# A token layer's chunk is issued in another order, beside and after another layer's convolutions

## The chip, the core and the metric

The kernel runs on one core of one Trainium2 chip, as one launch. The metric is device time in microseconds (us). The kernel before took 7097.66 us, the median of 3 runs between 7095.06 and 7098.18. The execution that the profiler recorded took 7082.74 us.

## The reference, cut to what matters

The input is `x` of 4 batches, 48 channels, 256 x 256 pixels, in float32. Four layers follow each other, each as `x = x + layer(groupnorm(x))`.

- Layer 0 is channel attention: a 1x1 and a 3x3 depthwise convolution make q, k and v; a 48 x 48 softmax of q against k weights v, and a 1x1 projection follows. Once the softmax of a batch is known, all of what lies behind it is one 3x3 convolution of the normalized input.
- Layer 1 is the token layer. It reads a batch's memory as tokens of 48 numbers, whatever pixels they came from:

```python
t = x.reshape(B, H * W, dim)
t = gelu(gelu(t @ W1 + b1))                 # 48 -> 16, exact gelu
x1, x2 = t[..., :8], t[..., 8:]
n = layernorm(x2)                           # over 8 features
sp = depthwise3x3(n as an image) + dw_b
ch = conv1x1(n as an image) + pw_b
out = (x1 * (sp * ch)) @ W2 + b2            # 8 -> 48, added to x
```

- Layers 2 and 3 are scans: each line of the image gets a 5-tap convolution of the line before it, down, up, right and left.

A layer starts with a group norm over whole batches, so layer 2 of a batch cannot start before layer 1 of that batch has ended. The scans take all four batches together.

## The kernel before

**Stages.** Layer 0's sums for the softmax of all batches fill the time from 0 to about 1050 us. Then come layer 0's output convolutions: 64 blocks of 16 rows, 16 a batch. `block(u)` (L623) makes one block in two halves. A half is two calls of `full` (L630, 3 matmuls each, `py` L642) and one of `rest(q)` (L646, 6 matmuls on half of the array, L651), then for each of its two PSUM tiles an addition of the input (DVE, L665) and statistics for the next group norm (DVE, L666). Half 0 writes two tiles of the PSUM pool `spare` (2 banks), half 1 two of the pool `banks` (5 banks). Between blocks ScalarE normalizes the next block's rows, `x1n` and `x2n` (L599), each in a single buffer, after the matmuls that read the old ones.

The blocks of batch 0 run alone. From about 1186 us the blocks of batches 1 to 3 run between the pieces of the token layer, whose 32 chunks (8 a batch, 32 rows each) follow one batch behind. When the blocks are used up (about 2359 us), the rest of the chunks runs alone until about 2737 us, and the scans take the rest. I call the first of these the **mixed stage**, the second the **lone stage**.

**A tick.** `tick(c, conv, alone)` (L985) works on three chunks: it transposes chunk c+1, makes the features of chunk c, and the output of chunk c-2 (`old`). `alone` is true when no half block is left. The pieces of one chunk are

- `load` (L799): two DMAs of 768 KB bring the chunk's tokens into `tok`, which has one buffer; `relay` (L807): GpSimd copies them to `pairs`, one buffer.
- `transposed(c, i)` (L814), i from 0 to 5: TensorE turns a sixth (4 matmuls into a bank, `ptok` L818); odd i are copied out by ScalarE (L822), even i by DVE (L824), into `xt`.
- `hidden` (L828): the projection `t @ W1` for each half of the features, 8 matmuls `ph` (L765); the eighth reads the `xt` of i = 5. ScalarE applies the two gelus (L835, L844, L846).
- `centered` (L849): a matmul `pm` (L852) makes the mean, DVE subtracts it (L854), GpSimd squares (`sq`, L856).
- `normed` (L858): a matmul `pvar` (L861), ScalarE's square root `v` (L863), DVE's reciprocal (L864) and product (L866), and ScalarE writes the image `n` (L868). Then ScalarE's queue starts four DMAs of 8 KB, `near<-n` (L878 to L887): each chunk's first and last row goes to its neighbours.
- `shift` (L889): GpSimd makes three shifted copies `nears` of a chunk's `near` (L891). That of chunk c-2 needs the third DMA of chunk c-1.
- `gate` (L893): three matmuls over `n` (`psp`, L897), one over `nears` (L898), one for the 1x1 convolution (`pch`, L900); then ScalarE (L903), DVE (L904) and GpSimd make the product `g` (L906).
- `output(c, ip, alone)` (L923), ip 0 and 1: four matmuls `pout` (L936), each on a quarter of the array's rows and each in a bank of its own, eight additions of the input `xr` on DVE (L946), eight copies of `y` to `yr` on GpSimd (L951), and after ip 1 the store `x2r<-yr` (L963) on SP's queue. `add_b2` (L919) has ScalarE add the bias to `xr`, which `load_x` (L908) loads.
- `finish` (L975): statistics on DVE (L979).

A mixed tick holds four half blocks. Its pieces stand in this order: the two `hidden`, `gate` of c-2, half block A, `centered`, transposes 0 and 1, `output` 0, half block B, transposes 2 and 3, `normed`, `output` 1, half block C, transposes 4 and 5, half block D. A and C are halves 0 and write `spare`.

**What sets the order.** The Tile framework records the pieces, and a scheduler of its own model of time lays down each engine's instructions in a fixed sequence; pieces given earlier have priority, but one that its model finds not ready is passed. On the chip each engine then runs its sequence in order. PSUM has eight banks: 5 `banks`, 2 `spare`, 1 for small things.

Of the kernel before, what the change touches and what calls it, by code (L numbers as in the profile page):

```python
# [9 lines left out]
F32 = mybir.dt.float32  # L10
# [8 lines left out]
P = 96  # L19
# [102 lines left out]
def layers01(ctx, tc, x, xp, xe, inside, pick, xc, x1, wqk, dwqk, wv, dwv, projT, temp, k, coef, coef1, gated, spare):  # L122
# [496 lines left out]
    stats = {}  # L619
    ends = []  # L620
    unwritten = []

    def block(u):  # L623

        b, n = items[u]
        if n == 0:
            stats[b] = small_p.tile([P, NB * 4, 6], F32, tag="st", name="st")
        held = {}

        def full(c):  # L630
            if c == 0:
                if u + 1 < len(items):
                    ahead_[u + 1] = load(items[u + 1])
                while unwritten:
                    unwritten.pop(0)()
                held["ps"] = {}
                held["w"] = [wy[b, i].rearrange("p x r o -> p x (r o)") for i in range(2)]
            ps = (banks if c % 2 else spare).tile([P, 2, W], F32, tag="bank", name="py")
            held["ps"][c] = ps
            x1n = ready[u][0]  # L640
            for dx in range(3):
                nc.tensor.matmul(  # L642
                    ps, lhsT=held["w"][0][:, dx], rhs=x1n[:, 2 * c : 2 * c + 2, dx : dx + W], start=dx == 0, stop=False
                )

        def rest(q):  # L646
            x2n = ready[u][1]
            for dx in range(3):
                for s in range(2):
                    here = slice(64 * s, 64 * s + 64)  # L650
                    nc.tensor.matmul(  # L651
                        held["ps"][q + 2 * s],
                        lhsT=held["w"][1][here, dx],
                        rhs=x2n[here, 2 * q : 2 * q + 2, dx : dx + W],
                        start=False,
                        stop=dx == 2,
                    )
            if q == 0:
                held["y"] = big.tile([P, M, W], F32, tag="y", name="y", bufs=2)
            elif u + 1 < len(items):  # L660
                ready[u + 1] = normed(items[u + 1], ahead_[u + 1])
            t1 = ahead_[u][0]
            for c in (q, q + 2):
                part = held["y"][:, 2 * c : 2 * c + 2, :]
                nc.vector.tensor_add(part, held["ps"][c], t1[:P, 2 * c : 2 * c + 2, :])  # L665
                nc.vector.bn_stats(stats[b][:, n * 4 + c, :], part.rearrange("p h w -> p (h w)"))  # L666
            if q == 0:
                return
            dst = x1[b].rearrange("c (h w) -> c h w", w=W)
# [21 lines left out]
        some_late()  # L691
    sctx.close()

    tick, n_ticks = gated(ctx, tc, banks, p_small)
    todo = [(u, q) for u in range(NB, len(items)) for q in range(2)]
    made = {}

# [15 lines left out]
            piece()  # L713


def gated_layer(ctx, tc, banks, p_small, x1, x2r, w1, w2, dw, ends, pw, cols, b2, k, coef1, coef2):

# [131 lines left out]
    def centered(c):  # L849
# [5 lines left out]
        sq = sqs[c] = feat.tile([128, CH], F32, tag="sq", name="sq", bufs=1)  # L855
        nc.gpsimd.tensor_mul(sq, d, d)  # L856

    def normed(c):  # L858
        b, j = items[c]
# [3 lines left out]
        nc.scalar.activation(v, pv, AF.Sqrt, bias=eps)  # L863
        nc.vector.reciprocal(v, v)  # L864
        d = ds.pop(c)
        nc.vector.tensor_mul(d, d, v)  # L866
        n = n_sb[c % NN]
        nc.scalar.activation(  # L868
            n[:, :, 1 : W + 1].rearrange("p k (t q) -> p k q t", q=4),
            by_token(d),  # L870
            AF.Identity,
            bias=col[:, 3:4],
            scale=col[:, 2:3],
        )

        here, a, z = near[c % NN], slice(0, F), slice(F, 2 * F)
        top, last = n[0:F], n[128 - F : 128]
        nc.scalar.dma_start(here[a, 1, :], last[:, 0, :])  # L878
        nc.scalar.dma_start(here[z, 0, :], top[:, 1, :])
        if j == 0:  # L880
            nc.scalar.dma_start(here[a, 0, :], zeros)
        else:
            nc.scalar.dma_start(near[(c - 1) % NN][z, 1, :], top[:, 0, :])
        if j == NJ - 1:
            nc.scalar.dma_start(here[z, 1, :], zeros)
        else:
            nc.scalar.dma_start(near[(c + 1) % NN][a, 0, :], last[:, 1, :])  # L887
# [35 lines left out]
    def output(c, ip, alone):  # L923
        b, j = items[c]
        if ip == 0:

            yrs[c] = res.tile([P, 8, 4, 128], F32, tag="yr", name="yr")
            if j == 0:
                stats[b] = feat.tile([P, NJ * 8, 6], F32, tag="st", name="st1")
        y = ys[c, ip] = res.tile([P, 2, 4, W], F32, tag="y1", name="y1")  # L930
        t, g = xrs[c, ip], gs[c]
        ps = []
        for q in range(4):
            p = banks.tile([P, 2, W], F32, tag="bank", name="pout")
            here = slice(32 * q, 32 * q + 32)
            nc.tensor.matmul(  # L936
                p,
                lhsT=w2_sb[here, ip, :],
                rhs=g[here],
                start=True,  # L940
                stop=True,
            )
            ps.append(p)
        for q in range(4):
            for kk in range(2):
                nc.vector.tensor_add(y[:, q % 2, 2 * kk + q // 2, :], ps[q][:, kk], t[:, 4 * kk + q, :])  # L946
        if alone:
            load_x(c + 1, ip)
        for i2 in range(2):
# [16 lines left out]
                )  # L966

        unwritten.append(write)
        if alone:
            unwritten.pop()()  # L970

    after = []
    unwritten = []
# [11 lines left out]
    def tick(c, conv, alone):  # L985
# [30 lines left out]
        if was:  # L1016
            pieces.append(lambda: gate(old))
        pieces.append(conv)
        if now:
            pieces.append(lambda: centered(c))  # L1020
        if new:
            pieces += [lambda i=i: transposed(c + 1, i) for i in range(2)]
        if was:
            pieces += [lambda: [add_b2(old, ip) for ip in range(2)], lambda: output(old, 0, alone)]
        pieces.append(conv)
        if new:
            pieces += [lambda i=i: transposed(c + 1, i) for i in range(2, 4)]
        if was:
            pieces.append(lambda: finish(old, 0))
        if now:  # L1030
            pieces.append(lambda: normed(c))
        if was:
            pieces.append(lambda: output(old, 1, alone))
        pieces.append(conv)
        if new:
            pieces += [lambda i=i: transposed(c + 1, i) for i in range(4, NI)]
        if was:
            pieces.append(lambda: finish(old, 1))
        pieces += [conv, last]
# [506 lines left out]
def program(ctx, tc, a, out, at):  # L1546
# [13 lines left out]
    def gated(ctx, tc, banks, p_small):  # L1560
        names = ("w1", "w2", "dw", "ends", "pw", "cols", "b2")
        to = [coef2[:, b] for b in range(B)]
        return gated_layer(ctx, tc, banks, p_small, x1, x2r, *(a[n] for n in names), k, coefs[1], to)
# [141 lines left out]
```

## Time and profile before

| What | Value |
|---|---|
| profiled execution | 7082.74 us, span 7080.7 us |
| runs | 7095.06, 7097.66, 7098.18 us |
| mixed ticks with all pieces, 1338.0 to 2358.9 us | 20 ticks, 51.0 us each |
| lone stage, 2358.9 us to the last store at 2736.4 us | 377.5 us |
| scans from the first matmul at 2745.2 us | 4335 us |
| TensorE busy over the span | 6631.8 us, 94% |
| DVE, ScalarE, GpSimd busy | 3644.3, 1854.5, 2086.7 us |

PE is TensorE's matmuls, PEld its weight loads, ACT is ScalarE, POOL is GpSimd, and SPq and ACTq are DMA issues on the queues of SyncE and ScalarE. L897 is line 897 of the kernel before. A line of the timeline gives start in us, duration in us, engine, line, operation, tiles, shapes, the count that was merged and, in brackets, the idle time before it and what ended that. PEclk is the granted clock of TensorE as a share of full speed. A line of the waits gives who waited for whom, the total in us, how often, and the longest.

### The profile page before, as it was taken

Reading aid. Unit: us, or ns where it says so; the run is one execution under the profiler, and the core shown is the slowest. Engines: PE = TensorE matmul, PEld = TensorE weight load, DVE = VectorE, ACT = ScalarE, POOL = GpSimd, SP = SyncE. Lnnn points to the kernel's source line nnn. Section 1 sums busy time; section 2 is a strip of 40 time slices with the busy share of each in tenths; the row PEclk is TensorE's granted clock in tenths of the full one; section 3 lists DMA queues with packets and bytes.
Section 4 is the critical chain, followed back from the end, with each engine's and each line's share of the span. In section 5 each row is a group of like instructions: output and inputs, shape, how many; then the busy total and the mean of one; then the engine's idle time right before and its main releaser. Section 6 shows DMA issues by size and latency. Waiting matters only on the chain.

```text
span 7080.7 us, 133914 instructions
## 1 busy us (share of the span) xinstructions
PE 6631.8 (94%) x55886; PEld 5328.3 (75%) x55886; DVE 3644.3 (51%) x8754; ACT 1854.5 (26%) x2166; POOL 2086.7 (29%) x4211
## 2 busy tenths in 40 slices
PE   4999999999999866999998999987899999899999
PEld 3766643333333325999998999986898999899999
DVE  6777623455555554444444445754344444444444
ACT  2440012344444443443441000001354344000000
POOL 0000000233333455330002556663000000455777
PEclk9999999999999877999999999998999999999999
DMA  7752145566666676995577778988997466865775
GB/s 195 188 151 82 52 134 155 166 188 184 192 183 183 153 175 193 278 299 143 184 215 185 199 196 163 254 241 210 186 165 134 130 193 188 221 191 176 274 289 203
DMA packets 1177647, 1325.90 MB, mean 187 GB/s; under 512 B 831344, under 2 KB 1006064, under 8 KB 1124688
## 3 DMA queue, kind: packets, MB, share of 16 engines
q1 hardware_dynamic: 1164016, 1229.16, 64.3%
q10 hardware_dynamic: 12928, 87.83, 3.7%
q8 instruction: 439, 7.19, 0.4%
q14 instruction: 168, 1.38, 0.1%
q0 software_dynamic: 96, 0.33, 0.0%
HBM read 793.94 MB, written 522.19 MB: 186 GB/s over the span
## 4 chain that ended last, share of the span: by engine, by line
PE 57%; SPq 3%; DMA 3%; DVE 2%; POOL 1%; issue 1%; ACT 1%; ACTq 0%; POOLq 0%; DVEq 0%
PE ps L1151 56%; SPq L1187 2%; DMA D<-d 1%; DMA tok<-x 1%; ACT d L1226 1%; POOL s L1436 1%; DVE y L946 0%; POOL yr L951 0%; PE ph L765 0%; DVE v L864 0%; DMA near<-n 0%; DVE st L979 0%; DMA r<-R 0%; PE pout L936 0%; PE psp L897 0%
## 5 line engine op out<-in xcount | busy, mean ns | idle before, releaser
L1151 PE MATMUL ps<-d,w 128*128 128x128 f32 (+1 forms) x18360 | 2071.2, 276 | 99.7 <-DVE d L1157 61.9
L1151 PEld LDWEIGHTS ps<-d,w 128*128 128x128 f32 x18360 | 2066.4, 193 | 104.3 <-DVE d L1157 65.7
L1151 PE MATMUL ps<-r,w 128*128 128x128 f32 (+1 forms) x18360 | 2072.1, 276 | 68.9 <-POOL r L1368 35.7
L1151 PEld LDWEIGHTS ps<-r,w 128*128 128x128 f32 x18360 | 2066.3, 193 | 74.7 <-DVE r L1157 37.5
L1157 DVE SCALAR_TENSOR_TENSOR d<-ps,b,d 128x128 f32<-128x128 f32 x3054 | 979.3, 348 | 1154.0 <-PE ps L1151 1073.8
L1436 POOL TENSOR_TENSOR s<-s,r 128x128 f32<-128x128 f32 x1536 | 748.6, 522 | 332.4 <-DVE r L1157 329.9
L1157 DVE SCALAR_TENSOR_TENSOR r<-ps,b,pre 128x128 f32<-128x128 f32 x1530 | 489.9, 348 | 582.2 <-PE ps L1151 581.3
L1157 DVE SCALAR_TENSOR_TENSOR r<-ps,b,r 128x128 f32<-128x128 f32 x1530 | 489.8, 348 | 460.0 <-PE ps L1151 429.7
L324 PE MATMUL acc<-moving,raw 128*32 128x240 f32 (+1 forms) x6144 | 687.9, 382 | 11.5 <-DVE moving L307 11.5
L642 PE MATMUL py<-x1n,wy 128*96 128x512 f32 x1536 | 696.6, 602 | 1.9
L1368 POOL COPY pre<-c 128x128 f32<-128x128 f32 x1530 | 559.8, 405 | 467.5 <-DVE r L1157 464.7
L324 PE MATMUL acc<-moving,still 128*32 128x240 f32 (+1 forms) x6144 | 684.5, 382 | 6.0 <-DVE still L311 2.3
L1226 ACT ACTIVATE d<-x,spread 128x256 f32<-128x256 f32 x752 | 511.2, 827 | 544.0 <-DMA D<-d 378.1
L1307 ACT COPY u<-d 128x384 f32<-128x384 f32 x510 | 451.3, 904 | 570.7 <-DVE d L1157 509.7
L324 PEld LDWEIGHTS acc<-moving,raw 128*32 128x32 f32 x6144 | 431.5, 110 | 185.6 <-DVE moving L307 11.8
L642 PEld LDWEIGHTS py<-x1n,wy 128*96 128x96 f32 x1536 | 243.7, 164 | 413.8 <-issue 371.0
L1368 POOL COPY r<-c 128x128 f32<-128x128 f32 x6 | 2.4, 399 | 1688.9 <-DMA c<-U 1688.9
L665 DVE TENSOR_TENSOR y<-py,t 96x512 f32<-96x512 f32 x256 | 173.2, 676 | 558.8 <-PE py L651 558.8
L324 PEld LDWEIGHTS acc<-moving,still 128*32 128x32 f32 x6144 | 371.8, 110 | 35.8 <-DVE still L311 3.2
L951 POOL COPY yr<-y 96x256 f32<-96x256 f32 x512 | 316.4, 662 | 201.6 <-DVE y L946 191.1
L651 PE MATMUL py<-x2n,wy 64*96 64x512 f32 x1536 | 360.8, 601 | 0.0
L651 PEld LDWEIGHTS py<-x2n,wy 64*96 64x96 f32 x1536 | 116.5, 158 | 233.4 <-issue 229.3
(204 smaller groups left out, 4213.8 us busy)
## 6 DMA issues: line engine op xcount, KB each, us to landing
t<-in_xc SPq DMA_DIRECT2D x64, 1536.0 KB
c<-U SPq DMA_DIRECT2D x348, 256.0 KB
D<-d SPq DMA_DIRECT2D x54, 1536.0 KB
d<-D SPq DMA_DIRECT2D x54, 1536.0 KB
R<-r SPq DMA_DIRECT2D x54, 1536.0 KB
r<-R ACTq DMA_DIRECT2D x54, 1536.0 KB
U<-u SPq DMA_DIRECT2D x84, 768.0 KB
raw<-in_xp SPq DMA_DIRECT2D x36, 1728.0 KB
```

The source lines that it names most:

```text
L324: nc.tensor.matmul(out[32 * i : 32 * i + 32, : n * C], lhsT=still[i][:, first : first + 32], rhs=moving[:, i, lo : lo + n * C], start=u == ...
L642: nc.tensor.matmul(ps, lhsT=held["w"][0][:, dx], rhs=x1n[:, 2 * c : 2 * c + 2, dx : dx + W], start=dx == 0, stop=False)
L651: nc.tensor.matmul(held["ps"][q + 2 * s], lhsT=held["w"][1][here, dx], rhs=x2n[here, 2 * q : 2 * q + 2, dx : dx + W], start=False, stop=dx ...
L665: nc.vector.tensor_add(part, held["ps"][c], t1[:P, 2 * c : 2 * c + 2, :])
L951: nc.gpsimd.tensor_copy(yrs[c][:, :, 2 * i2 + ip, :].rearrange("p j (n a g) -> p j n a g", a=4, g=4)[:, :, :, al], y[:, i2, al].rearrange( ...
L1151: nc.tensor.matmul(ps[m][:, here], lhsT=w[:, n, :], rhs=old[:, q, there], start=first, stop=last)
L1157: nc.vector.scalar_tensor_tensor(new[:, m], ps[m], bias[:, m : m + 1], inp[:, m], ALU.add, ALU.add)
L1187: queues[q % len(queues)].dma_start(v[p0 : p0 + np_, m, 8 * n0 : 8 * n1], src[c0:c1, 8 * n0 : 8 * n1, at : at + 64])
L1226: pin(nc.scalar.activation(dst, src, AF.Identity, bias=g[:, 1:2], scale=g[:, 0:1]))
L1307: nc.scalar.copy(v[:, :, i, :, al], line)
L1368: nc.gpsimd.tensor_copy(dst[:, m].rearrange("p (J a b) -> p J a b", J=NBK, b=B), v[:, m, j, :, gl].rearrange("p J b a -> p J a b"),)
L1436: nc.gpsimd.tensor_add(v, v, line[:, m].rearrange("p (J a b) -> p J a b", J=NBK, b=B))
```

## The change

Only the order of work and two choices of buffers change; every chunk is computed as before. In both stages:

- `gate` of c-2 still follows `hidden`, and `add_b2` stands right behind it.
- `normed` now ends with the square root; the reciprocal, the product and `n` are a piece of their own, `scaled`, and the four `near` DMAs another, `neighbours`. Both stand at the end of the tick, behind half block D and the last transpose.
- `output` is given in two parts of two `pout` each.
- The statistics of a half block (L666) are held back in the list `behind` until the next half block's first `full`.

In the mixed stage `output` 0 follows half block A and `centered`, transposes 0, 1, 3, 4, 2 stand together behind B, `pvar` and `output` 1 follow C, and transpose 5 follows D. In the lone stage every second `pout` takes a bank of `spare`, `output` 1 takes its `y` from the pool `big`, which layer 0 used until then, and a chunk's store stands behind the load of the next tokens, where it was issued as soon as it was made.

```diff
         def full(c):
+            if c < 2:
+                while behind:
+                    behind.pop(0)()
...
                 nc.vector.tensor_add(part, held["ps"][c], t1[:P, 2 * c : 2 * c + 2, :])
-                nc.vector.bn_stats(stats[b][:, n * 4 + c, :], part.rearrange("p h w -> p (h w)"))
+                behind.append(
+                    lambda c=c, part=part: nc.vector.bn_stats(
+                        stats[b][:, n * 4 + c, :], part.rearrange("p h w -> p (h w)")
+                    )
+                )
...
         nc.scalar.activation(v, pv, AF.Sqrt, bias=eps)
+        vs[c] = v
+
+    def scaled(c):
+        v = vs.pop(c)
         nc.vector.reciprocal(v, v)
         d = ds.pop(c)
         nc.vector.tensor_mul(d, d, v)
...
+    def neighbours(c):
+        b, j = items[c]
+        n = n_sb[c % NN]
         here, a, z = near[c % NN], slice(0, F), slice(F, 2 * F)
         top, last = n[0:F], n[128 - F : 128]
         nc.scalar.dma_start(here[a, 1, :], last[:, 0, :])
...
-        y = ys[c, ip] = res.tile([P, 2, 4, W], F32, tag="y1", name="y1")
...
+        if i == 0:
+            if alone and ip:
+                ys[c, ip] = big.tile([P, 2, 4, W], F32, tag="y", name="y1", bufs=2)
+            else:
+                ys[c, ip] = res.tile([P, 2, 4, W], F32, tag="y1", name="y1")
...
-        for q in range(4):
-            p = banks.tile([P, 2, W], F32, tag="bank", name="pout")
+        for q in (2 * i, 2 * i + 1):
+            ps[q] = (spare if alone and q % 2 else banks).tile([P, 2, W], F32, tag="bank", name="pout")
...
         unwritten.append(write)
-        if alone:
-            unwritten.pop()()
...
         def last():
             if c + 2 < n:
                 load(c + 2)
+            while alone and unwritten:
+                unwritten.pop(0)()
...
+        pieces += of_old(gate)
+        if alone:
+            pieces += [conv] + of_now(centered) + turned(0, 1) + added + out(0)
+            pieces += turned(3, 4) + of_old(finish, 0) + of_now(normed) + out(1) + turned(2, 5)
+        else:
+            pieces += [*added, conv, *of_now(centered), *out(0), conv]
+            pieces += turned(0, 1, 3, 4, 2) + of_old(finish, 0)
+            pieces += [conv, *of_now(normed), *out(1), conv, *turned(5)]
+        pieces += of_now(scaled) + of_now(neighbours) + of_old(finish, 1)
+        pieces.append(last)
```

More of the change, by code (lines that the diff above doesn't have):

```diff
@@ L621, in layers01 @@
     unwritten = []
+    behind = []
     def block(u):
@@ L665, in rest @@
                 nc.vector.tensor_add(part, held["ps"][c], t1[:P, 2 * c : 2 * c + 2, :])
-                nc.vector.bn_stats(stats[b][:, n * 4 + c, :], part.rearrange("p h w -> p (h w)"))
+                behind.append(
[3 more added lines that the diff above has]
+                )
             if q == 0:
                 return
+            while behind and n == NB - 1:
+                behind.pop(0)()
             dst = x1[b].rearrange("c (h w) -> c h w", w=W)
@@ L692, in layers01 @@
     sctx.close()
-    tick, n_ticks = gated(ctx, tc, banks, p_small)
+    tick, n_ticks = gated(ctx, tc, banks, p_small, big)
     todo = [(u, q) for u in range(NB, len(items)) for q in range(2)]
@@ L713, in layers01, with gated_layer @@
             piece()
-def gated_layer(ctx, tc, banks, p_small, x1, x2r, w1, w2, dw, ends, pw, cols, b2, k, coef1, coef2):
+def gated_layer(ctx, tc, banks, p_small, big, spare, x1, x2r, w1, w2, dw, ends, pw, cols, b2, k, coef1, coef2):
     nc = tc.nc
@@ L856, in centered @@
         nc.gpsimd.tensor_mul(sq, d, d)
+    vs = {}
     def normed(c):
-        b, j = items[c]
         pv = banks.tile([128, CH], F32, tag="bank", name="pvar")
@@ L921, in add_b2, with output @@
         nc.scalar.activation(t, t, AF.Identity, bias=b2_sb)
-    def output(c, ip, alone):
+    def output(c, ip, i, alone):
         b, j = items[c]
-        if ip == 0:
+        if ip == 0 and i == 0:
             yrs[c] = res.tile([P, 8, 4, 128], F32, tag="yr", name="yr")
@@ L929, in output @@
                 stats[b] = feat.tile([P, NJ * 8, 6], F32, tag="st", name="st1")
-        y = ys[c, ip] = res.tile([P, 2, 4, W], F32, tag="y1", name="y1")
-        t, g = xrs[c, ip], gs[c]
-        ps = []
-        for q in range(4):
-            p = banks.tile([P, 2, W], F32, tag="bank", name="pout")
+        if i == 0:
[3 more added lines that the diff above has]
+                ys[c, ip] = res.tile([P, 2, 4, W], F32, tag="y1", name="y1")
+        y, t, g = ys[c, ip], xrs[c, ip], gs[c]
+        ps = {}
+        for q in (2 * i, 2 * i + 1):
+            ps[q] = (spare if alone and q % 2 else banks).tile([P, 2, W], F32, tag="bank", name="pout")
             here = slice(32 * q, 32 * q + 32)
             nc.tensor.matmul(
-                p,
+                ps[q],
                 lhsT=w2_sb[here, ip, :],
@@ L942, in output @@
             )
-            ps.append(p)
-        for q in range(4):
+        for q in ps:
             for kk in range(2):
                 nc.vector.tensor_add(y[:, q % 2, 2 * kk + q // 2, :], ps[q][:, kk], t[:, 4 * kk + q, :])
+        if i == 0:
+            return
         if alone:
@@ L1015, in tick @@
             pieces += [lambda: hidden(c, 1), lambda: hidden(c, 0)]
[L1016 to L1039, printed above, removed]
+        turned = lambda *which: [lambda i=i: transposed(c + 1, i) for i in which] if new else []
+        out = lambda ip: [lambda i=i: output(old, ip, i, alone) for i in range(2)] if was else []
+        of_now = lambda f: [lambda: f(c)] if now else []
+        of_old = lambda f, *more: [lambda: f(old, *more)] if was else []
+        added = of_old(lambda c: [add_b2(c, ip) for ip in range(2)])
+        pieces += of_old(gate)
[8 more added lines that the diff above has]
+        pieces.append(last)
         if c == n + 1:
@@ L1558, in program, with gated @@
     x2r = [dram.tile([8 * C, 8, 1024], F32, tag=f"x2r_{b}", name=f"x2r_{b}") for b in range(B)]
-    def gated(ctx, tc, banks, p_small):
+    def gated(ctx, tc, banks, p_small, big):
         names = ("w1", "w2", "dw", "ends", "pw", "cols", "b2")
         to = [coef2[:, b] for b in range(B)]
-        return gated_layer(ctx, tc, banks, p_small, x1, x2r, *(a[n] for n in names), k, coefs[1], to)
+        return gated_layer(ctx, tc, banks, p_small, big, spare, x1, x2r, *(a[n] for n in names), k, coefs[1], to)
     names = ("wqk", "dwqk", "wv", "dwv", "projT", "temp")
```

## The prediction, made before the result

> **What bounds the kernel now.** I read the page's slices first, for whether TensorE sets the time everywhere.
>
> ```profile
> span 7080.7 us, 133914 instructions
> ...
> PE   4999999999999866999998999987899999899999
> ...
> PEclk9999999999999877999999999998999999999999
> ```
>
> A slice is 177 us. TensorE is full nearly everywhere. The gap in slices 14 and 15 is the lone stage (2358.9 to 2736.4 us). The change touches only the mixed ticks left of that gap and the gap itself. Next I read each engine's busy time by stage (mixed ticks, lone stage, its last 90 us).
>
> ```profile
> core 0: us, PE busy (x) PEld busy (x) DVE busy (x) ACT busy (x) POOL busy (x), PEclk, DMA share, GB/s
> 1338.00:2307.80 969.80, 960.84 (x3484) 359.39 (x3482) 540.86 (x933) 398.05 (x385) 329.37 (x590) 0.99 0.68 186
> 2358.90:2646.20 287.30, 193.93 (x788) 78.36 (x786) 160.82 (x295) 127.68 (x147) 145.58 (x199) 0.81 0.70 160
> 2646.20:2736.40 90.20, 49.73 (x114) 16.01 (x114) 41.83 (x88) 22.88 (x21) 41.92 (x67) 0.63 0.51 139
> ```
>
> In the mixed ticks TensorE is idle for 9 us of 970: any wait put in front of it there lengthens the tick by its whole length, and only fewer or shorter TensorE stretches shorten it. In the lone stage no engine is full; a chain of waits sets the time. Of the waits of the mixed stage, two matter, both on the small DMAs `near`:
>
> ```profile
> POOL nears L891 <- DMA near<-n: 106.9, 14, 12.3
> ...
> ACT xt L822 <- DMA near<-n: 47.9, 10, 5.8
> ```
>
> They cost nothing today, since TensorE has other work. How much room they have, the timelines of ScalarE, DVE, GpSimd and TensorE in the tick of 1712 us tell.
>
> ```profile
> 1726.44 3.35 DVE L864 RECIPROCAL v<-v 128x512 f32<-128x512 f32 x1 [1.32 <-ACT v L863]
> ```
> ```profile
> 1730.70 1.34 ACT L868 ACTIVATE n<-d,col 128x512 f32<-128x512 f32 x1 [4.29 <-DVE d L866]
> 1732.07 0.66 ACTq L878 DMA_DIRECT2D near<-n  x1
> 1732.77 0.63 ACTq L879 DMA_DIRECT2D near<-n  x1
> 1733.44 0.63 ACTq L883 DMA_DIRECT2D near<-n  x1
> 1734.10 3.48 ACTq L887 DMA_DIRECT2D near<-n  x1
> 1737.62 0.59 ACT L822 COPY xt<-ptok 128x512 f32<-128x512 f32 x1 [5.58 <-DMA near<-n]
> ```
> ```profile
> 1742.24 1.91 POOL L891 COPY nears<-near 16x512 f32<-16x512 f32 x3 [9.30 <-DMA near<-n]
> ```
> ```profile
> 1725.49 7.09 PE L642 MATMUL py<-x1n,wy 128*96 128x512 f32 x12
> ...
> 1752.32 1.02 PE L898 MATMUL psp<-nears,ends_sb 80*128 80x512 f32 x2
> ```
>
> The reciprocal starts 1 us into half block C; the third `near` issue ends at 1734.07, `nears` starts 8.2 us later and ends at 1744.15, and TensorE asks for it (L898) at 1752.32. Two half blocks' time lies between, with 8 us of slack here, about 6 us as the median of the ticks. From the third issue's end to `nears` the mixed ticks show 4.5 to 9.1 us, median 6.6; the lone ones 4.3 to 6.3.
>
> **Mixed tick, what is saved.** I compared the two fixed sequences engine by engine. A `pout` today waits for a bank, so 4 take 2.0 us behind A's work and 3.0 behind B's; on banks long free, 4 take 1.0. But B must wait for the bank of `pm`, free when DVE has written `d`, 2.75 us after A (4.0 today, with two transposes at 1.0). Behind B the five transposes take 2.4. Behind C, `pvar` and four `pout` take 2.0, and D waits until 3.35 for its bank, held until DVE's additions have read it. Transpose 5 takes 0.45. Without any new wait that is 8.95 us between half blocks against 9.8: a gain of 0.85 us per tick.
>
> **Mixed tick, what is new.** The reciprocal does not stand "behind the sums" in the sequence: it is between two groups of additions. I count from T, the end of half block C. DVE: two additions and two statistics (0.59 to 0.72 and 0.61 each) 2.5; four additions at 0.34 to 3.9; reciprocal 3.3 to 7.2; four additions to 8.55; product 0.65 to 9.2. ScalarE: `n` 1.35 to 10.6. Then the sequence has `x1n` (2.05, to 12.65) **ahead of** the four `near` issues: the third ends at 14.6, the fourth at 15.25 if it takes 0.65 (today it often takes 3 us and more, as in the line above: then 17.6). Then `x2n` 1.23 and the copy of transpose 5, 0.56: `xt` is ready at T+17.05 (19.4).
>
> TensorE: D runs from 3.35 to 11.4, transpose 5 to 11.85. The eighth `ph` reads that `xt` and is due at 13.45: **a first stall of 3.6 us** (6.0 with the slow fourth issue). Today the transposes stood ahead of D, and D covered their copies.
>
> GpSimd: in its sequence the first `nears` copy waits for `near`, and `relay` (two copies, 2.87 us) is between the first `nears` and the other two. With the median 6.6 us `near` lands at 21.2; 0.63 + 2.87 + 1.28 make `nears` ready at T+26.0 (23.7 with 4.3 us, 28.5 with 9.1). Without stalls TensorE would ask at 18.1 (11.85 + `ph` 3.5 + `psp` 2.75), with the first stall at 21.7: **a second stall of 4.3 us**. All of the 7.9 us is TensorE's, for conv A is queued behind L898. While GpSimd's `nears` waits, `relay` and so the next transposes queue behind it; those come behind half block B now, 16 us later, and are not late.
>
> From T to the next T: 26.0, L898 and `pch` 1.8, A 8.0, gap 2.75, B 8.1, transposes 2.4, C 8.1: 57.15 us. To this comes the granted clock. In the lone stage, the idle stretch from 2466.9 to 2469.1 us is followed by this stretch:
>
> ```profile
> 2469.70:2473.10 3.40, 3.40 (x17) 0.50 0.01 2
> ```
>
> The 17 matmuls there ran at half clock. Each mixed tick gets idle stretches as long as that one; a window of 3.4 us at half clock would cost up to 1.7 us, at least nothing where the next stall swallows it. I take 0.85: **58.0 us a tick against 51.05**, +7.0. Two of the 20 ticks belong to the last chunk of a batch, whose `near` has had a tick's time longer: there only the first stall stands, +2.8 each. The two shorter ticks ahead of 1338 us get about 2 each. 18 x 7.0 + 5.6 + 4 = **+136 us**.
>
> By the Trainium skill's page "DMA: Bandwidth & Descriptors", section "Anatomy of one DMA — SWDGE (gpsimd) path", a DMA's fixed cost is about 2.0 us, measured there for GpSimd's queue. By that figure `near` would land at 16.6, the second stall would vanish, and the sum would be that of the first rival; the rows above, 4.3 to 9.1 us for the same 8 KB, speak against it.
>
> **Held-back statistics, `add_b2` behind the gate.** 0.61 us each, on engines with 44% and 59% idle time; the next group norm needs the last ones only at a batch's end. Nothing; at worst one DVE statistic more ahead of `pm`'s product, 0.61 x 20 = 12 us.
>
> **Lone stage.** Its chain shows where its time goes.
>
> ```profile
> 2422.44 14.47 DMA tok<-x
> ...
> 2483.88 5.30 DMA near<-n
> 2489.19 8.88 DMA tok<-x
> ```
>
> Every second tick waits for tokens that queue behind the last store: TensorE idles 7.5 to 13 us there, and a pair of ticks takes 63.7 us, 31.8 each. Behind the change, the token loads go out first on SP's queue and this wait goes. Late next is a loop through one tick, since g of the next chunk needs `nears`: from g, DVE's contiguous work is 15.4 us (16 additions at 0.34, statistics 6 x 0.61, three copies 1.8, reciprocal 3.3, product); n 1.35; `near` behind `h` 2; landing 4.3 to 6; `nears` 1.9; L898 0.9; `sp` on two engines 1.5; g 1.3. That is 30 to 34 us, 32 taken: the token wait is replaced, not won. From 2358.9 to the g of chunk 29 I get 20 + 9 x 32 = 308 (today 302.5). From there to the last store's end 62 for 75, since `g` of the last two chunks no longer waits for a store to be issued. 370 against 377.5: **-7 us** (-30 to +15). At the end 10 instead of 7 input pieces load for the scans behind that store, while 12 others still go ahead of it, landing every 1.28 us: 0 (-3 to +5).
>
> **Sum.** +136 - 7 = +129 on the profiled execution's 7082.74: 7212. The runs' median is 14.9 above that execution: **7227 us**.
>
> **Rivals.**
> 1. *`near` lands within about 2 us*, or `relay` slips away from between the copies, so that only `xt` binds. L898 comes at T+21.7, the tick is 52.85, +1.8. 18 x 1.8 + 6 + 4 - 7 = +35: 7133. For it: in the profile the landing includes GpSimd's own lateness. Against: GpSimd's waits name the DMA 14 times.
> 2. *Slower still*: landing 9.1 us and a full half-clock window, tick 57.15 + 2.5 + 1.7 = 61.35, +10.3. 18 x 10.3 + 10 - 7 = +188: 7286; with the lone stage at its worst, 7300.
> 3. *Faster*: the lone loop is not bound by its chain, and falls to its DMA share, 0.70 x 31.8 = 22.3 us a tick. Nine ticks give 86, the tail 13; the mixed ticks at their lowest (landing 4.3, no half clock: 54.85, +3.8) cost 18 x 3.8 + 10 = 78. 7077. It decides once a lone tick is under 24.6 us. Against it: the 15.4 us of DVE in a row and the landing are rows of this trace, in one loop.
> 4. *The change doesn't do what it says*: "reciprocal behind sums" is half done already; if the transposes' or `pout`s' banks are not free either, 0.85 is lost, +15. It lies within the forecast's range.
>
> **How the numbers follow.** Forecast 7227, chance 0.62; its own range is 7188 to 7273 (landing -41 to +45, half clock +/-15, lone -23 to +22, added as squares). Rival 1 0.12, rival 2 0.12, rival 3 0.09, between them no change 0.05. About 0.2% is what a measurement of this kernel can tell from no change. So faster 0.09, same 0.05, slower 0.86. The range goes from 7115, below rival 1, to 7300.
>
> **What would show it.** In the changed kernel's profile: TensorE's idle time ahead of `ph` ended by ScalarE's `xt`, 2 to 6 us; ahead of L898's counterpart ended by GpSimd's `nears`, 3 to 6 us; clean mixed ticks of 56 to 60 us; `near` behind `x1n`; four `pout` in 1.0 us; no token wait in the lone chain and ticks of 30 to 34. A mixed tick under 52 us, or TensorE not waiting on `nears`, proves the second stall wrong; lone ticks under 25 prove the loop wrong.

## The result, and the profile after

The changed kernel takes 7252.94 us (median of 5 runs, 7251.06 to 7261.37), the kernel before 7097.66 (5 runs, 7080.98 to 7101.55). The ratio is 1.0226, with a 95% interval from 1.0211 to 1.0241. The forecast was 7227 in a range of 7115 to 7300. The profiled execution of the changed kernel has a span of 7251.2 us, 170.5 more than that of before. The medians differ by 155.3 only: the execution of before that was profiled is 15 us faster than that kernel's median, that of the changed kernel is the median itself. So some 15 of the 170.5 us are not due to the change, and where they lie isn't known.

The page of the changed kernel, its slices and the granted clock:

```profile
PE   4999999988888775999999999996898999899999
...
PEclk9999999999999866999999999998898999999999
```

A slice is 181 us here. TensorE, full before until the lone stage, is a tenth down in slices 8 to 12: these are the mixed ticks. In the slices that hold the lone stage (a part of 13, then 14 and 15) it is busy 7, 7 and 5 tenths, where the two lowest were 6, and the clock falls to 6 tenths from 7. Busy time by stage (mixed ticks, lone stage), as shown of before:

```profile
core 0: us, PE busy (x) PEld busy (x) DVE busy (x) ACT busy (x) POOL busy (x), PEclk, DMA share, GB/s
1338.00:2425.70 1087.70, 957.38 (x3502) 349.17 (x3500) 539.42 (x935) 394.30 (x385) 339.51 (x597) 0.96 0.59 164
2483.60:2852.00 368.40, 245.73 (x859) 98.08 (x858) 183.17 (x332) 146.28 (x164) 167.24 (x235) 0.70 0.56 128
```

In the mixed ticks TensorE idles for 130 us of 1088, where it idled for 9 of 970. In the lone stage its clock is 0.70, where it was 0.81.

To split the 170.5 us, I take in each trace the starts of L898 (L916 in the changed kernel), once a chunk: 20 mixed ticks lie from the first to the 21st, and the lone stage from the 21st to the scans' first matmul.

| kernel | median, us | ratio to before, 95% | mixed tick | lone stage |
|---|---|---|---|---|
| before | 7097.66 | | 51.05 | 380.0 |
| changed | 7252.94 | 1.0226 [1.0211, 1.0241] | 57.63 | 405.3 |
| e1 normed behind B | 7138.89 | 1.0059 [1.0044, 1.0074] | 52.19 | 405.1 |
| e2 transpose 5 behind B | 7232.95 | 1.0191 [1.0175, 1.0207] | 56.50 | 412.7 |
| e3 lone change only | 7111.65 | 1.0020 [1.0011, 1.0029] | 51.62 | 393.6 |
| e4 mixed change only | 7227.53 | 1.0181 [1.0164, 1.0198] | 58.03 | 375.9 |
| e5 both behind B | 7063.30 | 0.9956 [0.9942, 0.9969] | 50.03 | 376.0 |
| e6 store behind loads only | 7076.67 | 0.9972 [0.9958, 0.9986] | 51.62 | 365.8 |
| e7 filled waits | 7228.48 | 1.0189 [1.0175, 1.0203] | 58.01 | 382.2 |
| e9 e5 and e6 | 7053.54 | 0.9940 [0.9927, 0.9952] | 49.86 | 366.0 |
| e10 e9, normed first | 7069.31 | 0.9962 [0.9948, 0.9975] | 50.12 | 381.6 |
| e11 changed, normed first | 7246.45 | 1.0217 [1.0203, 1.0231] | 57.76 | 402.8 |
| e12 late near only | 7126.61 | 1.0037 [1.0024, 1.0051] | 52.00 | 395.5 |
| e13 banks and split only | 7113.61 | 1.0023 [1.0013, 1.0032] | 51.54 | 399.1 |

Ticks and stages are of one profiled execution each. From before to the changed kernel: the first L898 comes 7.0 us later, 20 ticks of 6.58 more make 131.7, the lone stage 25.3, the scans 6.4: 170.4. In all traces here the scans take 4334 to 4346 us, so their 6.4 is no sign of the change. Nor is half a microsecond a tick: in e6 the mixed stage is that of before, and its ticks took 51.62 us for 51.05.

TensorE's waits over the changed mixed stage, who waited for whom, total, count and longest:

```profile
PE ph L775 <- ACT xt L832: 90.0, 20, 6.9
...
PE psp L916 <- POOL nears L909: 3.4, 2, 1.7
```

The first wait is there 20 times; the second, forecast at 4.3 us a tick, hardly at all. The tick of half block C's end at 1440.1 us says why. ScalarE, with its DMA issues, then TensorE, then GpSimd:

```profile
1449.45 1.33 ACT L883 ACTIVATE n<-d,col 128x512 f32<-128x512 f32 x1 [5.02 <-DVE d L881]
1450.58 2.05 ACT L599 ACTIVATE x1n<-t,g 128x2048 f32<-128x2048 f32 x1
1450.81 0.63 ACTq L896 DMA_DIRECT2D near<-n  x1
1451.47 0.63 ACTq L897 DMA_DIRECT2D near<-n  x1
1452.13 3.17 ACTq L901 DMA_DIRECT2D near<-n  x1
1455.35 2.41 ACTq L905 DMA_DIRECT2D near<-n  x1
1457.87 1.24 ACT L599 ACTIVATE x2n<-t,g 128x1024 f32<-128x1024 f32 x1 [5.23 <-issue]
1459.01 0.56 ACT L832 COPY xt<-ptok 128x512 f32<-128x512 f32 x1
```
```profile
1452.32 1.92 PE L775 MATMUL ph<-xt,w_sb 128*32 128x512 f32 x14
1459.63 4.87 PE L775 MATMUL ph<-xt,w_sb 128*32 128x512 f32 x18 [5.39 <-ACT xt L832]
...
1467.11 1.02 PE L916 MATMUL psp<-nears,ends_sb 80*128 80x512 f32 x2
```
```profile
1460.99 0.60 POOL L909 COPY nears<-near 16x512 f32<-16x512 f32 x1 [8.86 <-DMA near<-n]
...
1464.47 1.25 POOL L909 COPY nears<-near 16x512 f32<-16x512 f32 x2
```

The copy of transpose 5 stands behind the four issues, which took 6.95 us instead of 2.6. TensorE waits 5.4 us for it and then runs the rest of `ph` in 4.87 us. Behind the wait the granted clock was 0.50 (the columns are those of the stages). In another tick, where it stayed at 1.00, the same 18 records (a matmul here has two) took 2.76:

```profile
1459.90:1463.30 3.40, 3.40 (x17) 0.97 (x12) 0.00 (x0) 3.37 (x4) 2.31 (x3) 0.50 0.95 318
```
```profile
1745.12 2.76 PE L775 MATMUL ph<-xt,w_sb 128*32 128x512 f32 x18 [3.00 <-ACT xt L832]
```

Five of the 20 waits lasted 3.0 us or less and left the clock at 1.00; behind the other 15 it fell.

In the tick of 1440.1 TensorE asks for `nears` at 1467.1, 1.4 us after `nears` is ready (1465.7). Both waits are there; the second is hidden behind the first.

### The profile page after: what moved, and what is told of

It reads as the page before. It is cut to its first block, busy times and chain, and to the rows that moved or that the text cites. A ratio compares the mean times of both kernels' runs of the same rounds, so it can differ in the third digit from the quotient of the medians.

```text
span 7251.2 us, 133883 instructions
## 1 busy us (share of the span) xinstructions
PE 6652.0 (92%) x55886; PEld 5305.3 (73%) x55886; DVE 3643.3 (50%) x8754; ACT 1844.2 (25%) x2162; POOL 2090.2 (29%) x4211
## 4 chain that ended last, share of the span: by engine, by line
PE 80%; DVE 6%; DMA 5%; SPq 2%; POOL 2%; issue 2%; ACT 1%; ACTq 1%; POOLq 0%; DVEq 0%
PE ps L1165 54%; PE py L646 8%; PE acc L324 8%; PE py L655 4%; SPq L1201 2%; PE ph L775 1%; DVE y L669 1%; DVE v L879 1%; DMA near<-n 1%; DMA sx<-in_x 1%; PE pout L958 1%; POOL yr L974 1%; DVE y L967 1%; DMA D<-d 1%; PE psp L915 1%
## 5 line engine op out<-in xcount | busy, mean ns | idle before, releaser
L324 PEld LDWEIGHTS acc<-moving,still 128*32 128x32 f32 x6144 | 344.4, 110 | 36.5 <-DVE still L311 4.0
L599 ACT ACTIVATE x1n<-t,g 128x2048 f32<-128x2048 f32 x64 | 133.4, 2085 | 610.6 <-PE py L646 591.7
```

Source lines behind the costliest of these rows:

```text
L324: nc.tensor.matmul(out[32 * i : 32 * i + 32, : n * C], lhsT=still[i][:, first : first + 32], rhs=moving[:, i, lo : lo + n * C], start=u == ...
```

## The experiments

My theory after the result: in the mixed stage the loss is `normed` standing behind half block C instead of B, so that `near` is issued late, in front of the copy of transpose 5 and too late for `nears`; in the lone stage it is a loop of waits that got longer. The rivals: the transposes in a row and `pm`'s bank; for the lone stage, that it only inherits a late start.

**e1.** In the mixed stage:

```diff
             pieces += turned(0, 1, 3, 4, 2) + of_old(finish, 0)
-            pieces += [conv, *of_now(normed), *out(1), conv, *turned(5)]
+            pieces += of_now(normed) + of_now(scaled) + of_now(neighbours)
+            pieces += [conv, *out(1), conv, *turned(5)]
...
-        pieces += of_now(scaled) + of_now(neighbours) + of_old(finish, 1)
+        if alone:
+            pieces += of_now(scaled) + of_now(neighbours)
+        pieces += of_old(finish, 1)
```

> The changed kernel, but in the mixed stage pvar, the reciprocal, n and the near DMAs stand behind half block B and its transposes, as in the kernel before; the pouts, their banks, the transposes and the lone stage stay as changed. Theory 'late normed' (the stalls in the mixed tick come from the near DMAs being issued behind half block C's work instead of B's): near is issued about 10 us earlier, it no longer stands ahead of transpose 5's copy, and nears is ready before TensorE asks; a mixed tick falls from 58.1 to 49.0 to 50.0 us, and the total to 7253 - 18 x 8.5 = about 7100, up to 7115. Rival 'transposes and banks' (the five transposes together, pm's bank and transpose 5 behind D are what costs): the tick stays above 55 us and the total above 7200.

Measured: 52.19 us a tick, 7138.9. The rival is out, but my 49 to 50 missed too. `near` is early (its four issues take 0.63 us each, and `nears` is ready 13 to 19 us ahead of TensorE); yet in most ticks TensorE still waits about 2.5 us for the copy of transpose 5, now behind ScalarE's `add_b2` and `x2n`:

```profile
1444.69 4.19 PE L775 MATMUL ph<-xt,w_sb 128*32 128x512 f32 x18 [2.46 <-ACT xt L832]
```

So that transpose behind D costs by itself.

**e2.**

```diff
-            pieces += turned(0, 1, 3, 4, 2) + of_old(finish, 0)
-            pieces += [conv, *of_now(normed), *out(1), conv, *turned(5)]
+            pieces += turned(0, 1, 3, 4, 2, 5) + of_old(finish, 0)
+            pieces += [conv, *of_now(normed), *out(1), conv]
```

> The changed kernel, but in the mixed stage transpose 5 stands with the other five behind half block B. The first stall (TensorE's ph waits for ScalarE's copy of transpose 5) can't occur any more. In the fixed sequence GpSimd's relay also leaves its place between the nears copies. Theory 'late normed': nears then binds instead; third near issue at T+15.3, landing 5.7, nears 1.9, ready at T+22.9, and TensorE waits for it about 5 us; the tick goes from 58.1 to 54.5 to 56 us only, the total to about 7200 (7180 to 7220). Rival 'transpose 5 alone': nothing waits behind it, the tick falls to 49.5 to 50.5 us and the total to about 7100.

Measured: 56.50 us a tick, 7233. Taking the first wait away brings out the second, as the wait and one tick of it show:

```profile
PE psp L916 <- POOL nears L909: 81.0, 18, 6.4
```
```profile
1465.93 2.07 PE L916 MATMUL psp<-nears,ends_sb 80*128 80x512 f32 x2 [4.82 <-POOL nears L909]
```

The wait is 4.8 us, and L916 behind it takes 2.07 us instead of 1.02. Only 1.1 of the 6.6 us per tick came back: the two waits lie beside each other, not behind each other.

**e5** joins both moves, with the lone stage as before:

```diff
-            pieces += turned(0, 1, 3, 4, 2) + of_old(finish, 0)
-            pieces += [conv, *of_now(normed), *out(1), conv, *turned(5)]
-            pieces += of_now(scaled) + of_now(neighbours) + of_old(finish, 1)
+            pieces += turned(0, 1, 3, 4, 2, 5) + of_old(finish, 0)
+            pieces += of_now(normed) + of_now(scaled) + of_now(neighbours)
+            pieces += [conv, *out(1), *of_old(finish, 1), conv]
```

> Mixed stage as changed, but with pvar, reciprocal, n and near (as in e1) and transpose 5 (as in e2) both behind half block B; lone stage as in the kernel before. Theory 'two waits' (e1 and e2 each left one of the two waits of the changed tick: ScalarE's late copy of transpose 5, or late nears): with both gone, a mixed tick is the sum of its pieces, 3.6 + 4.4 + 8.0 + 1.1 + 1.7 + 8.1 + 3.2 + 0.9 + 8.0 + 1.0 + 8.1 = 48.1 to 49.5 us against 51.0 before, and the total 30 to 60 us below the kernel before (7040 to 7070). Rival 'banks' (the wait for pm's bank and the transposes in one row cost as much as the pouts on free banks save): tick 50 to 51.5, total within 15 us of the kernel before.

Measured: 50.03 us a tick, 7063.3, a ratio of 0.9956. With both waits gone the rest of the mixed change gains: 1.0 us a tick against before. That is more than executions differ by: the order of before took 51.05 to 52.00 us a tick in the five traces that have it (before, e3, e6, e12, e13), this order 49.86 to 50.12 in three (e5, e9, e10). The tick is still longer than the sum of its pieces, since the six transposes took 4.5 us instead of 3.2, `pvar` waiting 1.1 us for a copy to free a bank.

**e3 and e4** split the two stages. e3 gives the mixed stage the pieces of before in their order; e4 gives the lone stage its order, banks, buffers and stores of before. e3:

```diff
-            pieces += [*added, conv, *of_now(centered), *out(0), conv]
-            pieces += turned(0, 1, 3, 4, 2) + of_old(finish, 0)
-            pieces += [conv, *of_now(normed), *out(1), conv, *turned(5)]
+            pieces += [conv, *of_now(centered), *turned(0, 1), *added, *out(0), conv]
+            pieces += turned(2, 3) + of_old(finish, 0) + of_now(normed) + of_now(scaled) + of_now(neighbours)
+            pieces += [*out(1), conv, *turned(4, 5), *of_old(finish, 1), conv]
-        pieces += of_now(scaled) + of_now(neighbours) + of_old(finish, 1)
+        if alone:
+            pieces += of_now(scaled) + of_now(neighbours) + of_old(finish, 1)
```

e4, with its outputs of four `pout` and its stores at once, as before:

```diff
-            ps[q] = (spare if alone and q % 2 else banks).tile([P, 2, W], F32, tag="bank", name="pout")
+            ps[q] = banks.tile([P, 2, W], F32, tag="bank", name="pout")
...
-            pieces += turned(3, 4) + of_old(finish, 0) + of_now(normed) + out(1) + turned(2, 5)
+            pieces += turned(2, 3) + of_old(finish, 0) + of_now(normed) + of_now(scaled) + of_now(neighbours)
+            pieces += out(1) + turned(4, 5) + of_old(finish, 1)
```

> The mixed stage's pieces in the order of the kernel before, the lone stage as changed. Theory 'lone loop' (the lone stage itself became slower: g, DVE's work, n, near, nears, g, with TensorE at half clock in it): lone ticks of 34 to 37 us as in the changed kernel, total 25 to 30 us above the kernel before, about 7125. Rival 'inherited' (the lone stage is late only because the mixed stage hands it over late): lone ticks of 30 to 32, total within 10 us of the kernel before.

> The mixed stage as changed, the lone stage in the order and with the buffers and stores of the kernel before. If the two stages' shares add up: mixed ticks of 58 us and a lone stage as in the kernel before, total 125 to 140 us above the kernel before, about 7230. If they don't: under 7215 or over 7250.

e4 costs 131 us (7227.5 against 7096.4 on its chip), e3 15; the change as a whole 155. The mixed stage is the loss. The lone stage itself is longer in e3, by 13.6 us; 'inherited' is out as the only cause, though 11.7 us more come in the changed kernel, most of it in its first two lone ticks (70.8 us against 62.0 in e3). What hands them on was not tried. The held-back statistics cost nothing that shows: e3 has them, e6 has not, and the mixed ticks of both take 51.62 us.

**e6**, before with this alone:

```diff
         unwritten.append(write)
-        if alone:
-            unwritten.pop()()
...
                 load(c + 2)
+            while alone and unwritten:
+                unwritten.pop(0)()
```

> The kernel before, with one thing changed: in the lone stage a chunk's store is issued behind the next token load. Theory 'order, not store' (the loss of the lone stage comes from the reciprocal standing behind all the additions and from TensorE at half clock; the store behind the loads is a gain that the rest of the lone change uses up): the token waits of 7.5 to 13 us in every second tick go, ticks of 28 to 30 us where pairs took 63.7, total 20 to 45 us below the kernel before. Rival 'one loop anyway' (the prediction's: the token wait is replaced by the loop over near): ticks of 31 to 33, total within 10 us of the kernel before, or the store itself is what loses, total above it.

Measured: 19 us faster (0.9972), the lone stage 14.2 shorter, but its steady ticks are 31 to 34 us, as the prediction's loop had it, not 28 to 30. The store is a gain; the change uses it up elsewhere.

**e12 and e13** start from e6 and add one half each of the rest of the lone change: e12 the late reciprocal, product, `n` and `near`; e13 the spare banks, the other pool and the output in two parts. Both keep the held-back statistics. Seen from e3, the lone order of e12, which also has the banks, the `y` and the whole outputs of before, is

```diff
-            pieces += turned(3, 4) + of_old(finish, 0) + of_now(normed) + out(1) + turned(2, 5)
+            pieces += turned(2, 3) + of_old(finish, 0) + of_now(normed) + out(1) + turned(4, 5)
```

and that of e13

```diff
-            pieces += turned(3, 4) + of_old(finish, 0) + of_now(normed) + out(1) + turned(2, 5)
+            pieces += turned(2, 3) + of_old(finish, 0) + of_now(normed) + of_now(scaled) + of_now(neighbours)
+            pieces += out(1) + turned(4, 5) + of_old(finish, 1)
...
-        if alone:
-            pieces += of_now(scaled) + of_now(neighbours) + of_old(finish, 1)
```

> Mixed stage in the order of before, stores behind token loads as in e6, banks and whole outputs as before; of the lone change only this: reciprocal, product, n and near come at the end of the tick. In the fixed sequence 8 additions (2.7 us) and a copy now stand between the reciprocal and its product. If late near alone makes the changed lone tick long: ticks of 34 to 36 us where e6 has 31.4, total 20 to 40 us above e6, about 7107. If not: ticks of 31 to 33, within 12 us of e6.

> Mixed stage in the order of before, stores behind token loads as in e6; of the lone change only this: the spare banks, y in the other pool and the output in two parts; reciprocal, n and near are given right behind pvar as before. In the fixed sequence the free banks let 6 of the 8 pouts and 15 of the 16 additions go ahead of the reciprocal (8 additions and a few statistics in e6). If that is what makes the changed lone tick long: ticks of 34 to 36 us, total 20 to 40 us above e6, about 7107. If not: ticks of 31 to 33, within 12 us of e6.

Measured: e12 50 us above e6, e13 37; the lone stage is 30 and 33 us longer. Their steady ticks are 35.6 to 39.2 and 36.1 to 37.6 us. Together (e3) they are no worse than each alone. That fits two ways of lengthening one loop; it isn't shown by a row.

**e7**, the changed kernel with fillers in the lone ticks (`pch` written eight times, `pm` three times, with the same values; `pch` stands ahead of the matmul over `nears`, as it already runs in the changed kernel):

```diff
+        if alone:
+            for _ in range(8):
+                nc.tensor.matmul(pch, lhsT=pw_sb, rhs=n[:, :, 1 : W + 1], start=True, stop=True)
         nc.tensor.matmul(psp, lhsT=ends_sb, rhs=shifted[c % 2], start=False, stop=True)
...
-        nc.tensor.matmul(pm, lhsT=k["mean8", 128], rhs=h2, start=True, stop=True)
+        for _ in range(3 if alone else 1):
+            nc.tensor.matmul(pm, lhsT=k["mean8", 128], rhs=h2, start=True, stop=True)
```

> The changed kernel, with pch computed eight times over and pm three times over in the lone ticks (the same values written again), so that TensorE works through its waits for nears and for g. Theory 'half clock' (the lone tick became 35.5 instead of 32 us because TensorE comes out of each wait at half clock, and L916, the pouts and the transposes of the loop take twice their time): the first pouts take 1.0 instead of 2.0 us, the lone ticks fall to 31.5 to 33.5 us, total 20 to 35 us below the changed kernel, about 7225. Rival 'only DVE and DMA' (the loop's time is DVE's and the DMAs'; TensorE's clock is hidden beside them): ticks stay at 35 to 36 us and the total within 8 us of the changed kernel, or above it where the extra work is in the way.

The lone window of the result section, in e7:

```profile
2483.60:2852.00 368.40, 316.05 (x1080) 130.05 (x1082) 187.65 (x344) 148.00 (x165) 170.78 (x241) 0.86 0.57 130
```

The granted clock goes from 0.70 to 0.86, the lone stage from 405.3 to 382.2 us, the total 24 us below the changed kernel. The first two `pout` behind `g` take 1.1 us instead of 2.0. More work on TensorE made the kernel faster: its half clock was in the loop.

**e9** is e5 with e6's store.

> e5 and e6 in one kernel: normed and all transposes behind half block B in the mixed stage, stores behind token loads in the lone stage in its order of before. If the two gains add up: the sum of what e5 and e6 measure, 50 to 100 us below the kernel before. If the lone stage can't use an earlier hand-over: no better than e5 by over 10 us.

Measured: 7053.5, a ratio of 0.9940 [0.9927, 0.9952]. The gains add in part (32 and 19 make 42). It beats both kernels.

**e10 and e11** put `normed`, `scaled` and `neighbours` right behind `centered` in the lone ticks, of e9 and of the changed kernel:

```diff
-            pieces += [conv] + of_now(centered) + turned(0, 1) + added + out(0)
+            pieces += [conv] + of_now(centered) + of_now(normed) + of_now(scaled) + of_now(neighbours)
+            pieces += turned(0, 1) + added + out(0)
```

> e9, and in the lone stage pvar, reciprocal, n and near stand right behind centered, ahead of all of output. Theory 'loop through the outputs' (the lone tick is the loop g, pouts and their additions, pvar, reciprocal, n, near, nears, g; how much of output stands ahead of pvar and of the reciprocal sets the tick): the loop shrinks to sp 0.75, d 0.67, reciprocal 3.3, product 0.65, n 1.35, issues 2, landing 4.5 to 6, nears 1.9, L898 1 to 2, sp 0.7, g, or else to DVE's 12.3 us from sp to the last xt copy and TensorE's 8 to 9 behind it, 20 to 23 us; lone ticks fall from 31.4 to 23 to 26 us, the total 45 to 75 us below e9, about 6995. Rival 'no loop' (the ticks are bound by the token and input loads or by GpSimd's copies, which this leaves alone): ticks of 30 us and more, total within 15 us of e9.

> The changed kernel, mixed stage untouched; in the lone stage pvar, reciprocal, n and near stand right behind centered, ahead of all of output; its banks, buffers, split output and store stay as changed. Theory 'loop through the outputs' (the changed lone tick takes 35.7 us because three quarters of the pouts and 12 to 16 additions stand between g and the next reciprocal): lone ticks of 24 to 28 us, total 65 to 100 us below the changed kernel, about 7170. Rival 'banks and buffers' (the spare banks, the y in the other pool or the split output cost the time): ticks stay above 33 us, total within 20 us of the changed kernel.

Both missed: e10 is 16 us slower than e9 (lone stage 381.6 against 366.0), e11 within 7 of the changed kernel. `near` is early in e10, but TensorE now waits elsewhere:

```profile
2510.65 1.69 PE L872 MATMUL pvar<-sq,cst 128*128 128x512 f32 x2 [2.77 <-POOL sq L866]
...
2517.90 2.02 PE L955 MATMUL pout<-g,w_sb 32*96 32x512 f32 x2 [2.59 <-DVE xt L834]
...
2522.32 1.97 PE L828 MATMUL ptok<-cst,pairs 128*128 128x128 f32 x8 [2.40 <-ACT xt L832]
```

The reciprocal and the issues now stand ahead of the copies `xt`, so the next chunk's features come later. My theory that the loop over `near` alone sets the lone tick is refuted: another of almost the same length must be right behind it. In e11 `relay` in GpSimd's sequence came to stand behind `nears` and waited with it. Which loop would be last if both were cut was not settled.

## Why the prediction was right, and where it was not

- **Direction, bottleneck and mixed tick: right.** The changed tick was put at 58.0 us; 15 of the 20 took 57.7 to 58.3, four beside a batch's end 53.7 to 55.6, the last 63.7. Up to the 21st L898 the loss is 138.7 (131.7 + 7.0) for the +136 of the sum; up to the end of the last half block, where the forecast drew the line (2358.9 before, 2483.1 now), it is 124. e4 and e5 show the cause as named: with `normed` and transpose 5 back behind B the loss is a gain.
- **Partly luck.** The sum took before's mean, 51.05, from a clean tick of 58.0. A clean tick of before takes 49.7 to 50.0 (ten of the 20; the others 50.9 to 54.4), so a clean tick lost 8.2 us, not 7.0. Two short ticks more than forecast, and long ticks of before that did not come back, made up for it. The total of 7253 for 7227 holds a mixed stage that was met and a lone stage that was missed.
- **The two stalls: the sum right, the split wrong.** 3.6 + 4.3 was forecast. Measured in the tick shown are 5.4 for the first (forecast 6.0 with slow issues), 2.1 of half clock behind it (forecast 0.85, at most 1.7), and nothing for the second: `nears` was ready 1.4 us ahead of TensorE. By the prediction's own sign, TensorE not waiting on `nears`, the second stall is proved wrong for the changed kernel; e2 shows it, 4.8 us, once the first is gone.
- **The near issues behind `x1n`: wrong, and made up for.** They ran beside `x1n` (1450.81, while it ran from 1450.58 to 1452.63), not behind it, but the third took 3.17 instead of 0.65. The third ended at T+15.2; 14.6 was forecast. Its landing took 5.7 for the median 6.6.
- **The 0.85 us saved per tick: not there.** From the last matmul of a half block to the first behind its gap, the stretches of the changed tick are 2.7, 2.6, 3.55 and 0.5: 9.3 us for the forecast 8.95. Those of before, measured alike, are 3.9, 4.8, 0.9 and none: 9.5 for the 9.8 of the forecast. The gain is 0.15 us.
- **The lone stage: wrong.** -7 was forecast and +25.3 came by the table, +36 between the forecast's own ends (413 us from the last half block to the last store, for 377.5); in e3 it is +13.6. The token wait went, as said; what failed is the step "from g, DVE's contiguous work is 15.4 us". It is not contiguous: TensorE's pouts stand in between, at half clock (granted 0.50 from 2681.2 to 2692.0). TensorE's tick in the changed kernel, and DVE's between `g` and the reciprocal:

```profile
2676.11 2.07 PE L916 MATMUL psp<-nears,ends_sb 80*128 80x512 f32 x2 [7.70 <-POOL nears L909]
2681.15 2.02 PE L958 MATMUL pout<-g,w_sb 32*96 32x512 f32 x4 [2.97 <-POOL g L924]
2684.10 2.65 PE L958 MATMUL pout<-g,w_sb 32*96 32x512 f32 x4 [0.93 <-DVE y L967]
...
2688.58 2.02 PE L958 MATMUL pout<-g,w_sb 32*96 32x512 f32 x4
```
```profile
2683.21 1.41 DVE L967 TENSOR_TENSOR y<-pout,xr 96x256 f32<-96x256 f32 x4 [3.52 <-PE pout L958]
...
2690.64 1.41 DVE L967 TENSOR_TENSOR y<-pout,xr 96x256 f32<-96x256 f32 x4 [1.26 <-PE pout L958]
...
2694.59 1.41 DVE L967 TENSOR_TENSOR y<-pout,xr 96x256 f32<-96x256 f32 x4 [0.75 <-PE pout L958]
...
2696.52 3.34 DVE L879 RECIPROCAL v<-v 128x512 f32<-128x512 f32 x1
```

  g ends at 2681.1; the first addition starts 2.1 us later, and three gaps of 0.4, 1.3 and 0.7 us follow. That is 4.5 us on top of DVE's work (15.7 here), and L916 takes 2.07 for the 0.9 of the sum. From this g to the next (2716.7) are 35.6 us. The sum itself was added up wrongly: its terms make 28.7 to 30.4, not 30 to 34, and with 4.5 and 1.2 more 34.4 to 36.1. e7 shows the half clock's part: with the waits filled the lone stage is 23 us shorter. The tail was mis-sized as well: from the end of g of chunk 29 (2822.1) to the last store 74 us, as before (75), for the forecast 62. Next to nothing was won there: the last two g end 15.9 us apart, 16.9 before.
- **Rivals and range.** "`near` lands early" is out (5.7 us in the tick shown), though its picture, a wait for `xt` alone, is what the profile shows. "Slower still" needed ticks of 61.35, "faster" lone ticks under 24.6: those of the changed kernel took 27.1 to 38.3, the last one aside, and no kernel here had a steady mean under 31. "The change doesn't do what it says" came true in part: of the 0.85 us, 0.15 is there. Added as squares, the terms of the forecast's own range give 7178 to 7279, not 7188 to 7273; 7253 lies in both.

## What to carry to other kernels

Two waits that lie beside each other look like one in the profile: the later one shows only once the first is taken away, and moving either alone returned 1.1 to 5.4 of the 6.6 us per tick, both together 7.6. A chain "of one engine's work" is to be walked with every engine that feeds it, at the clock that the waits before it leave. And a fixed place in one engine's queue is dear for what stands behind: four small DMA issues delayed a copy of 0.56 us, and with it TensorE.

## What of the hardware was not expected

ScalarE's queue started DMA issues while its own activation was still running (0.23 us after the start of a 2.05-us `x1n`). Four issues of the same kind took 2.6 us in e1's ticks and 6.95 in the changed kernel's, 12 us later in the tick, counted from half block C's end. What slows them was not tried; in the tick shown they stand beside issues of SyncE's queue that are slow too (2.04 us at 1453.90, two in 3.34 at 1455.98), and in e1 no `near` issue overlaps one of that queue. The length of a wait alone did not tell whether the clock fell: in the changed mixed stage waits of up to 3.0 us left it at 1.00, and behind one of 2.46 us in e1 it was 0.64 over the next 3.4 us. Filling TensorE's waits with needless matmuls took 24 us off the changed kernel.
